# First complex product of two spectral layers in three real products, its activations read one item later

## The chip, the core and the metric

The kernel runs on one core of a Trainium2 chip. The metric is the device time of one execution in microseconds (us), here the median of several executions. The engines are named as in the profile: PE is TensorE (matrix products; PEld is the loading of its stationary operand), DVE is VectorE, ACT is ScalarE, POOL is GpSimd, SP is SyncE, which issues most DMAs. Engines work on tiles in SBUF and PSUM; a product's result arrives in PSUM.

## The reference

Four layers follow one another on an array x of 48 x 48 positions with 768 channels in float32: a transformer block (attention with relative positions, then an MLP), a spectral layer, a scan with a small convolution, and a second spectral layer. The change touches only the two spectral layers, which are the same up to their weights:

```python
xs = jnp.fft.rfft2(xf32, axes=(1, 2)).reshape(B, H, Wm, NUM_HEADS, BLOCK)   # 48 x 25 modes, 8 blocks of 96
xr, xi = jnp.real(xs), jnp.imag(xs)
o1r = relu(einsum('bxyhi,hio->bxyho', xr, w1[0]) - einsum('bxyhi,hio->bxyho', xi, w1[1]) + b1[0])
o1i = relu(einsum('bxyhi,hio->bxyho', xi, w1[0]) + einsum('bxyhi,hio->bxyho', xr, w1[1]) + b1[1])
o2r = einsum('bxyho,hoi->bxyhi', o1r, w2[0]) - einsum('bxyho,hoi->bxyhi', o1i, w2[1]) + b2[0]
o2i = einsum('bxyho,hoi->bxyhi', o1i, w2[0]) + einsum('bxyho,hoi->bxyhi', o1r, w2[1]) + b2[1]
out_c = softshrink(zr, LAMBDA) + 1j * softshrink(zi, LAMBDA)     # zr, zi: o2r, o2i
return jnp.fft.irfft2(out_c, s=(H, W), axes=(1, 2)) + bias       # bias is the layer's input
```

So each of the 8 blocks of 96 channels passes through a complex MLP of two layers, mode by mode. The first of its complex products, xr + i xi with w1[0] + i w1[1], is what the change computes in another way.

## The kernel before, in words

A spectral layer has three stages. First `spectrum_rows` takes the transform along one axis of the picture as products on TensorE and stores it to DRAM (`yu`, one array for each half of the channels). Then `spectrum_mix` takes the transform along the other axis, the MLP, the soft shrinkage and the inverse transform along that axis, and stores back to `yu`. Then the rows are transformed back, in `afno_first` (L1510) for the first spectral layer and `afno_second` (L1541) for the second.

`spectrum_mix` works on items: 2 halves x 5 groups `kc` of KC = 5 modes x 4 blocks of channels, 40 items a layer. G is 48, so an item has n = KC * G = 240 complex columns, or CH = 480 real ones, on 96 partitions (BS). An item passes through four functions:

- `s_fft_h`: five products of 96x96 from the loaded tile `yt` (L1379) give the spectrum in PSUM; ScalarE copies it to `X` in SBUF, real and imaginary part apart (L1381). For the first block of a group it loads `yt` (720 KB) first.
- `s_mlp1`: four products of 96x240 (L1390 to L1393) give real and imaginary part of the first complex product in PSUM, two of them accumulated for each. `w1n` (L1362) holds -w1[1]. ScalarE applies bias and Relu to each part (L1396) into planes 1 and 2 of the tile `o1`; GpSimd writes plane 0 as the negative of plane 2 (L1397).
- `s_mlp2`: ten products of 97x96 (L1407, L1408) with `o1` as the stationary operand give the second complex product, with the bias as a 97th row. The pairs of planes 1, 2 and 0, 1 are the operand for w2[0] and w2[1]. VectorE clamps the result to +-LAMBDA (`cl`, L1411) and subtracts the clamp from it (`Z`, L1413), which is the soft shrinkage.
- `s_ifft_h`: one product of 96x480 (L1422); in the first layer VectorE adds `yt` (L1425), in the second ScalarE and VectorE copy in turn (`ev`, L57 and L59) into `us`, which is stored after the fourth block (L1429).

The order of the instructions is that in which the program emits them; each engine works through its own queue in that order and waits on semaphores for its operands. The order is a software pipeline written out in the last loop: in each step the stages come in reversed order, and stage s works on item step - s.

```python
        stages = [s_fft_h, s_mlp1, s_mlp2, s_ifft_h]
        for step in range(len(items) + len(stages) - 1):
            for s in reversed(range(len(stages))):
```

So TensorE's queue has, step by step, the inverse transform of the item three behind, the second product of the item two behind, the first product of the item one behind, and the forward transform of the new item. Of `o1` there are two tiles in turn, of `X`, `cl`, `Z`, `yt` and `us` two each. PSUM has eight tiles (tag "m") in turn for the whole layer; an item takes four.

Names and lines that matter below: L1322 the products of `spectrum_rows` (f_f), L1353 the load of `yt`, L1033 an add for the scan layer (the tiles `bias` and `u`) whose loads and add lie at the beginning of the first spectral layer's mixing stage, L1158 GpSimd's product in the scan, L1237 its complex products for the rotation, L139 GpSimd's preparation of weights in the transformer block, L564 VectorE's accumulation in the attention, L840 ScalarE's activation in the MLP, L884 GpSimd's add of the MLP's bias.

Of the kernel before, what the change touches and what calls it, by code (L numbers as in the profile page):

```python
# [11 lines left out]
F32 = mybir.dt.float32  # L12
BF16 = mybir.dt.bfloat16
AF = mybir.ActivationFunctionType
ALU = mybir.AluOpType
# [5 lines left out]
G = 48  # L21
# [7 lines left out]
TB = 384  # L29
# [7 lines left out]
NB, BS = 8, 96  # L37
KW = G // 2 + 1
KC = 5
# [95 lines left out]
def combine_right(eng, p, t1, t2, t3, t4):  # L135

    eng.tensor_tensor(t1, p[1], p[0], ALU.subtract)
    eng.tensor_tensor(t3, p[3], p[1], ALU.subtract)
    eng.tensor_tensor(t2, p[3], t1, ALU.subtract)  # L139
    eng.tensor_tensor(t4, p[2], t2, ALU.subtract)  # L140


def block_sums(nc, X, t1, t2, t4):


    blocks = [X[:, k * NC2 : (k + 1) * NC2, n, :] for k in range(2) for n in range(2)]
    combine_right(nc.vector, blocks, t1, t2, blocks[1], t4)
    return blocks[0], blocks[2], t2, t1, blocks[3], blocks[1], t4
# [32 lines left out]
def qkv_phase(tc, ident, x, qkv_w, qkv_b, relT, rel_d, ln_g, ln_b, q_d, k_d, v_d, rw_d, rh_d, wqk_d, wv_d, flag, ahead):  # L181
# [17 lines left out]
    with (  # L199
# [67 lines left out]
        def q_and_k(sb):  # L267
# [3 lines left out]
            for pr in range(NC):  # L271
# [49 lines left out]
                for o, d, m in ((q[:, pr], q_d, qms), (kt, k_d, kms)):  # L321
                    o = o.rearrange("p b t -> p (b t)")
                    nc.scalar.dma_start(d[pr * P : (pr + 1) * P, tok], o)
                    V.tensor_reduce(m[:, pr, sb : sb + 1], o, axis=AX.X, op=ALU.max, apply_absolute_value=True)
                if pr == NC2 and sb + 1 < NSB:
# [33 lines left out]
        with tc.tile_pool(name="qkv_o", bufs=1, side="right") as op:  # L359
# [80 lines left out]
            qm, km = (qp.tile([P, NC], F32, tag=n, name=n) for n in ("qm", "km"))  # L440
            V.tensor_reduce(qm, qms, axis=AX.X, op=ALU.max)
            V.tensor_reduce(km, kms, axis=AX.X, op=ALU.max)
            rm = qp.tile([P, 2], F32, tag="rm", name="rm")
            V.tensor_reduce(rm, rel, axis=AX.X, op=ALU.max, apply_absolute_value=True)
            V.tensor_scalar(km, km, rm[:, 0:1], rm[:, 1:2], ALU.add, ALU.add)
# [881 lines left out]
def spectrum_mix(tc, name, a, layer, yu, psum, keep, side, halves):  # L1327

    nc = tc.nc
    ev = Evac(nc)
    w1, b1, w2, b2 = (a[f"{layer}_{k}"] for k in ("w1", "b1", "w2", "b2"))
    HB = NB // 2
    with (
        tc.tile_pool(name=f"{name}_c", bufs=1, side=side) as cp,
        tc.tile_pool(name=f"{name}_y", bufs=2, side=side) as yp,
        tc.tile_pool(name=f"{name}_s", bufs=2, side=side) as sp,  # L1340
    ):
        fh = cp.tile([BS, BS], F32, tag="fh", name=f"{name}_fh")
        nc.sync.dma_start(fh, a["fh"])
        w1t = cp.tile([BS, NB, 2, BS], F32, tag="w1", name=f"{name}_w1")
        w1n = cp.tile([BS, NB, BS], F32, tag="w1n", name=f"{name}_w1n")
        w2t = cp.tile([BS + 1, NB, 2, BS], F32, tag="w2", name=f"{name}_w2")
        b1t = cp.tile([BS, 2, NB], F32, tag="b1", name=f"{name}_b1")
        ih = cp.tile([BS, BS], F32, tag="ih", name=f"{name}_ih")
        ys = {}

        def load(half, kc):
            yt = yp.tile([BS, KC, TB], F32, tag="yt", name=f"{name}_yt_{half}_{kc}")
            nc.sync.dma_start(yt, yu[half][4 * KC * kc : 4 * KC * (kc + 1)].rearrange("(k q) p c -> (q p) k c", q=4))  # L1353
            us = yp.tile([BS, KC, TB], F32, tag="us", name=f"{name}_us_{half}_{kc}")
            ys[half, kc] = yt, us

        nc.sync.dma_start(w1t, w1)
        nc.sync.dma_start(b1t, b1)
        nc.sync.dma_start(w2t[:BS], w2)
        nc.sync.dma_start(w2t[BS : BS + 1], b2)  # L1360
        nc.sync.dma_start(ih, a["ih"])
        nc.gpsimd.tensor_scalar(w1n, w1t[:, :, 1, :], -1.0, None, ALU.mult)  # L1362

        o1s = []
        for i in range(2):
            o1 = cp.tile([BS + 1, KC, 3, G], F32, tag=f"o1{i}", name=f"{name}_o1{i}")
            nc.vector.memset(o1[BS : BS + 1, :, :, :], 0.0)
            nc.vector.memset(o1[BS : BS + 1, :, 1, :], 1.0)
            o1s.append(o1)
        flow = {}  # L1370

        def s_fft_h(i):
            half, kc, b = items[i]
            if b == 0:
                load(half, kc)
            yt = ys[half, kc][0]
            ps = psum(f"x_{i}")
            for j in range(KC):
                nc.tensor.matmul(ps[:BS, j * BS : (j + 1) * BS], lhsT=yt[:, j, b * BS : (b + 1) * BS], rhs=fh, start=True, stop=True)  # L1379
            X = sp.tile([BS, 2, KC, G], F32, tag="X", name=f"{name}_X_{i}")  # L1380
            nc.scalar.copy(X, ps[:BS, :CH].rearrange("c (k r h) -> c r k h", r=2, h=G))  # L1381
            flow[i] = X

        def s_mlp1(i):
            half, kc, b = items[i]
            b += half * HB
            X = flow[i].rearrange("c r k h -> c r (k h)")
            ps = psum(f"o_{i}")
            n = KC * G
            nc.tensor.matmul(ps[:BS, :n], lhsT=w1t[:, b, 0, :], rhs=X[:, 0, :], start=True, stop=False)  # L1390
            nc.tensor.matmul(ps[:BS, :n], lhsT=w1n[:, b, :], rhs=X[:, 1, :], start=False, stop=True)
            nc.tensor.matmul(ps[:BS, n : 2 * n], lhsT=w1t[:, b, 0, :], rhs=X[:, 1, :], start=True, stop=False)
            nc.tensor.matmul(ps[:BS, n : 2 * n], lhsT=w1t[:, b, 1, :], rhs=X[:, 0, :], start=False, stop=True)  # L1393
            o1 = o1s[i % 2]
            for r in range(2):
                nc.scalar.activation(o1[:BS, :, 1 + r, :], ps[:BS, r * n : (r + 1) * n].rearrange("c (k h) -> c k h", h=G), AF.Relu, bias=b1t[:, r, b : b + 1])  # L1396
            nc.gpsimd.tensor_scalar(o1[:BS, :, 0, :], o1[:BS, :, 2, :], -1.0, None, ALU.mult)  # L1397
            flow[i] = o1

        def s_mlp2(i):  # L1400
            half, kc, b = items[i]
            b += half * HB
            o1 = flow[i]
            ps = psum(f"z_{i}")
            for j in range(KC):
                out = ps[:BS, j * BS : (j + 1) * BS]
                nc.tensor.matmul(out, lhsT=o1[:, j, 1:3, :].rearrange("c r h -> c (r h)"), rhs=w2t[:, b, 0, :], start=True, stop=False)  # L1407
                nc.tensor.matmul(out, lhsT=o1[:, j, 0:2, :].rearrange("c r h -> c (r h)"), rhs=w2t[:, b, 1, :], start=False, stop=True)  # L1408

            cl = sp.tile([BS, CH], F32, tag="cl", name=f"{name}_cl_{i}")  # L1410
            nc.vector.tensor_scalar(cl, ps[:BS, :CH], -LAMBDA, LAMBDA, ALU.max, ALU.min)  # L1411
            Z = sp.tile([BS, CH], F32, tag="Z", name=f"{name}_Z_{i}")
            nc.vector.tensor_tensor(Z, ps[:BS, :CH], cl, ALU.subtract)  # L1413
            flow[i] = Z

        def s_ifft_h(i):
            half, kc, b = items[i]
            Z = flow.pop(i)
            yt, us = ys[half, kc]
            cols = slice(b * BS, (b + 1) * BS)  # L1420
            ps = psum(f"u_{i}")
            nc.tensor.matmul(ps[:BS, :CH], lhsT=ih, rhs=Z, start=True, stop=True)  # L1422
            pv = ps[:BS, :CH].rearrange("p (k c) -> p k c", c=BS)
            if keep:
                nc.vector.tensor_tensor(us[:, :, cols], pv, yt[:, :, cols], ALU.add)  # L1425
            else:
                ev(us[:, :, cols], pv)
            if b == HB - 1:
                nc.sync.dma_start(yu[half][4 * KC * kc : 4 * KC * (kc + 1)].rearrange("(k q) p c -> (q p) k c", q=4), us)  # L1429

        items = [(half, kc, b) for half in halves for kc in range(NKC) for b in range(HB)]
        stages = [s_fft_h, s_mlp1, s_mlp2, s_ifft_h]
        for step in range(len(items) + len(stages) - 1):
            for s in reversed(range(len(stages))):
                i = step - s
                if 0 <= i < len(items):
                    stages[s](i)


def load_spectrum(nc, pool, yu, half, g, name):  # L1440
# [216 lines left out]
```

## Time and profile before

| | before |
|---|---|
| median of three executions | 3971.84 us (3970.29 to 3973.61) |
| profiled execution, span | 3971.0 us |
| mean granted TensorE clock | 0.973 |
| first spectral layer, first copy of X to last inverse transform | 2905.80 to 3123.3 us |
| second spectral layer, the same | 3712.81 to 3926.07 us |

The profile's page gives the busy time of each engine with its share of the span and its count of instructions, then the chain of work that ended last, followed back from the last instruction. The windows of busy time give the same for a stretch of the span. In the timeline a line is a group of neighbouring records of one kind: start and span in us, engine, line, operation, output <- inputs by the program's names, the shapes, the count, and in brackets how long the engine had been idle before and what released it. A float32 product leaves two records. The ends of matmuls are modelled, so starts are the better times for TensorE; spans on GpSimd are rough.

### The profile page before, as it was taken

How to read it: one execution, taken by the hardware profiler on the slowest of the kernel's cores; microseconds unless marked ns; L12 is line 12 of the kernel's file. 1: busy time of each engine (PE TensorE's matmuls, PEld its weight loads, DVE VectorE, ACT ScalarE, POOL GpSimd, SP SyncE). 2: the span in 40 equal slices, each digit the busy share in tenths (PEclk: the TensorE clock that was granted, in tenths of full speed). 3: DMA queues.
4: the chain of work that ended last, by engine and by line, in shares of the span. 5: the costliest groups of instructions: out<-in, count | busy, mean ns of one | idle time of the engine just before them, and what ended most of it. 6: DMA issues, size and time to landing. Idle time of an engine off the chain costs nothing.

```text
span 3971.0 us, 54147 instructions
## 1 busy us (share of the span) xinstructions
PE 3818.7 (96%) x22178; PEld 2329.6 (59%) x22178; DVE 2008.6 (51%) x3020; ACT 1093.3 (28%) x1808; POOL 595.6 (15%) x415
## 2 busy tenths in 40 slices
PE   7999869999999999999999999999989998998998
PEld 4666544444444444455555555555568866995685
DVE  6645446666666666556325233233223268994334
ACT  1323234444434444421210110120022135222331
POOL 3101001101011111034000000000011111971110
PEclk9999989999999999999999999999989799999999
DMA  7666463334232322224335434534434302110434
GB/s 247 195 196 185 157 168 104 101 101 129 78 112 80 104 88 72 86 80 162 106 112 161 142 103 126 156 107 125 128 97 103 94 18 91 38 32 23 144 100 157
DMA packets 262424, 457.24 MB, mean 115 GB/s; under 512 B 32413, under 2 KB 215701, under 8 KB 255799
## 3 DMA queue, kind: packets, MB, share of 16 engines
q1 hardware_dynamic: 251927, 431.07, 36.2%
q10 hardware_dynamic: 10240, 22.61, 1.5%
q8 instruction: 177, 2.90, 0.3%
q14 instruction: 80, 0.66, 0.1%
HBM read 315.31 MB, written 138.31 MB: 114 GB/s over the span
## 4 chain that ended last, share of the span: by engine, by line
PE 71%; issue 10%; DVE 8%; DMA 4%; POOL 3%; ACT 2%; SPq 1%; ACTq 0%; POOLq 0%; DVEq 0%
PE p L845 12%; PE p L908 12%; PE s L546 10%; PE av L575 10%; PE qk L293 6%; PE s L554 4%; PE c L1061 4%; PE v L164 3%; DVE rec L585 2%; PE so L1221 2%; POOL f_o L1397 2%; PE f_w L1510 2%; PE c L1150 1%; PE f_f L1322 1%; DVE s L1170 1%
## 5 line engine op out<-in xcount | busy, mean ns | idle before, releaser
L564 DVE TENSOR_TENSOR acc<-acc,p 128x768 f32<-128x768 f32 x576 | 585.5, 1016 | 357.2 <-ACT p L556 315.5
L556 ACT ACTIVATE p<-s 128x768 f32<-128x768 f32 x648 | 478.6, 812 | 709.3 <-PE s L554 709.3
L546 PE MATMUL s<-qt,kt 64*128 64x384 f32 x2592 | 478.9, 502 | 22.6 <-DVE rest_h L367 21.0
L908 PE MATMUL p<-w,h 128*128 128x384 f32 x1512 | 492.4, 486 | 0.0
L575 PE MATMUL av<-p,vt 128*64 128x384 f32 x2592 | 467.4, 496 | 19.1 <-DVE oT L586 11.5
L908 PEld LDWEIGHTS p<-w,h 128*128 128x128 f32 x1512 | 286.2, 190 | 196.8
L546 PEld LDWEIGHTS s<-qt,kt 64*128 64x128 f32 x2592 | 233.5, 187 | 264.5 <-ACT p L556 88.3
L575 PEld LDWEIGHTS av<-p,vt 128*64 128x64 f32 x2592 | 172.3, 137 | 240.7 <-issue 196.1
L845 PE MATMUL p<-x2nT,w 128*128 128x384 f32 x864 | 293.1, 489 | 0.7 <-issue 0.7
L1150 PE MATMUL c<-H,bands 128*48 128x96 f32 x5632 | 242.7, 247 | 12.3 <-issue 12.3
L554 PE MATMUL s<-bt,oneh 120*128 120x384 bf16 x1296 | 248.2, 328 | 0.0
L1150 PEld LDWEIGHTS c<-H,bands 128*48 128x48 f32 x5632 | 235.5, 124 | 19.7 <-issue 12.7
L293 PE MATMUL qk<-xnT,wqk 128*128 128x384 f32 x756 | 244.8, 486 | 0.0
L845 PEld LDWEIGHTS p<-x2nT,w 128*128 128x128 f32 x864 | 165.0, 191 | 116.4 <-issue 2.9
L845 PE MATMUL p<-xT,w 128*128 128x384 f32 x648 | 220.7, 486 | 0.0
L554 PEld LDWEIGHTS <-oneh 120*128 120x128 bf16 x1296 | 109.1, 98 | 173.6 <-issue 112.2
L293 PEld LDWEIGHTS qk<-xnT,wqk 128*128 128x128 f32 x756 | 143.4, 190 | 99.4
L840 ACT ACTIVATE h<-h,ml_b 128x384 f32<-128x384 f32 x144 | 88.4, 615 | 347.6 <-DVE h L860 176.6
L884 POOL TENSOR_TENSOR rr<-rr,ml_b 128x1152 f32<-128x1152 f32 x12 | 31.7, 2644 | 955.6 <-DMA rr<-xr_d 955.6
L845 PEld LDWEIGHTS p<-xT,w 128*128 128x128 f32 x648 | 123.1, 190 | 85.9
L1158 POOL TENSOR_TENSOR t<-s,c 128x768 f32<-128x768 f32 x80 | 144.8, 1835 | 172.2 <-DVE s L1120 160.5
L1061 PE MATMUL c<-wsc,x2T 128*112 128x357 f32 (+1 forms) x576 | 151.8, 426 | 2.0 <-DVE c L1022 2.0
(298 smaller groups left out, 4678.1 us busy)
## 6 DMA issues: line engine op xcount, KB each, us to landing
w<-w1s_d SPq DMA_DIRECT2D x36, 768.0 KB
w<-w2s_d SPq DMA_DIRECT2D x36, 768.0 KB
bt<-rh_d SPq DMA_DIRECT2D x144, 162.0 KB
w<-w1s_d SPq DMA_DIRECT2D x36, 576.0 KB
w<-in_mlp_w_dram SPq DMA_DIRECT2D x27, 768.0 KB
wqk<-wqk_d SPq DMA_DIRECT2D x12, 1344.0 KB
f_gt<-yu SPq DMA_DIRECT2D x24, 672.0 KB
bt<-rw_d SPq DMA_DIRECT2D x144, 108.0 KB
```

The costliest lines, as they stand in the source:

```text
L164: nc.tensor.matmul(p[:, :TB], lhsT=rhs[n][:, c, t * P : (t + 1) * P], rhs=w[:, c, :], start=c == 0, stop=c == NC2 - 1)
L293: nc.tensor.matmul(p[:, :TB], lhsT=w[:, n, c, :], rhs=ops[sb][n][:, c, :], start=c == 0, stop=c == NC2 - 1)
L546: nc.tensor.matmul(ps[:, s, :QB], lhsT=keys[pr][rows, kt * P : (kt + 1) * P], rhs=chunks[c][0][rows], start=True, stop=False)
L554: nc.tensor.matmul(ps[:, s, :QB], lhsT=oneh[:NBR, b % 3, :], rhs=chunks[c][1][:NBR, s, b // 3, j, :], start=False, stop=True)
L556: nc.scalar.activation(p, ps[:, :, :QB], AF.Exp)
L564: nc.vector.tensor_tensor(probs[c], probs[c], p, ALU.add)
L575: nc.tensor.matmul(avs[c][rows, :QB], lhsT=vals[pr][:, kt, rows], rhs=p[:, s, :], start=kt == 0, stop=kt == NT - 1)
L845: nc.tensor.matmul(p[:, :TB], lhsT=w[n][:, c, :], rhs=rhs[n][:, c, :], start=c == 0, stop=c == NC2 - 1)
L908: nc.tensor.matmul(ps[t][:, :TB], lhsT=hs[left, f][:, t * P : (t + 1) * P], rhs=wt[:, f % KW2, :], start=f == 0, stop=f == NF2 - 1)
L1061: nc.tensor.matmul(ps[:K, i, :n], lhsT=xT[:, cc, tok : tok + K], rhs=w[:, cc, c0 : c0 + n], start=cc == 0, stop=cc == NC - 1)
L1150: nc.tensor.matmul(ps[r0 : r0 + G, k // 4, cols], lhsT=bands[:, n - GC, i, :] if gr else bands0[:, n, i, :], rhs=H[:, n, :, d : d + NPR], ...
L1158: GP.tensor_tensor(t, sc[:, ch], c1[:, m0 : m0 + GC].unsqueeze(2).to_broadcast([P, GC, RR, NPR]), ALU.mult)
```

## The change

With Xs = xr + xi the two parts of the first product can be written with one product in common: real = w1[0].Xs - (w1[0] + w1[1]).xi and imaginary = w1[0].Xs + (w1[1] - w1[0]).xr. That is three real products instead of four, for additions ahead of them and behind them. The change does this for both layers:

- `w1n` is replaced by `w1s` = w1[0] + w1[1] and `w1d` = w1[1] - w1[0], two GpSimd operations of 96x768 a layer instead of one.
- `s_fft_h` has GpSimd add the two parts of `X` into `Xs` (L1384 of the new kernel).
- `s_mlp1` has three products: p2 with Xs (L1394), which needs a PSUM tile of its own, then those with xr and xi (L1395, L1396). ScalarE copies p2 to SBUF (`both`, L1399); VectorE forms the two parts (`pre`, L1400 and L1401) from `both` and the products in PSUM; Relu with bias (L1404) reads `pre` in SBUF instead of PSUM; the negation (L1405) stays.
- The second product works three items behind instead of two, and the inverse transform four instead of three, so that there is a step more between the Relus and their use. Of `o1` there are three tiles in turn, of `yt` three; a layer takes 44 steps instead of 43.

The order of stages within a step, inverse transform, second product, first product, forward transform, stays as it was. On GpSimd the sum Xs of an item comes in the queue behind the negation of the item before. The lines of the later instructions move: second product L1415 and L1416, clamp L1419, Z L1421, inverse transform L1430, add L1433, store L1437, rows of the first layer L1518.

```diff
-        w1n = cp.tile([BS, NB, BS], F32, tag="w1n", name=f"{name}_w1n")
+        w1s, w1d = (cp.tile([BS, NB, BS], F32, tag=n, name=f"{name}_{n}") for n in ("w1s", "w1d"))
...
-            yt = yp.tile([BS, KC, TB], F32, tag="yt", name=f"{name}_yt_{half}_{kc}")
+            yt = yp.tile([BS, KC, TB], F32, tag="yt", name=f"{name}_yt_{half}_{kc}", bufs=3)
...
-        nc.gpsimd.tensor_scalar(w1n, w1t[:, :, 1, :], -1.0, None, ALU.mult)
+        nc.gpsimd.tensor_tensor(w1s, w1t[:, :, 0, :], w1t[:, :, 1, :], ALU.add)
+        nc.gpsimd.tensor_tensor(w1d, w1t[:, :, 1, :], w1t[:, :, 0, :], ALU.subtract)
...
-        for i in range(2):
+        for i in range(3):
             o1 = cp.tile([BS + 1, KC, 3, G], F32, tag=f"o1{i}", name=f"{name}_o1{i}")
...
             nc.scalar.copy(X, ps[:BS, :CH].rearrange("c (k r h) -> c r k h", r=2, h=G))
-            flow[i] = X
+            Xs = sp.tile([BS, KC, G], F32, tag="Xs", name=f"{name}_Xs_{i}")
+            nc.gpsimd.tensor_tensor(Xs, X[:, 0], X[:, 1], ALU.add)
+            flow[i] = X, Xs
...
-            nc.tensor.matmul(ps[:BS, :n], lhsT=w1t[:, b, 0, :], rhs=X[:, 0, :], start=True, stop=False)
-            nc.tensor.matmul(ps[:BS, :n], lhsT=w1n[:, b, :], rhs=X[:, 1, :], start=False, stop=True)
-            nc.tensor.matmul(ps[:BS, n : 2 * n], lhsT=w1t[:, b, 0, :], rhs=X[:, 1, :], start=True, stop=False)
-            nc.tensor.matmul(ps[:BS, n : 2 * n], lhsT=w1t[:, b, 1, :], rhs=X[:, 0, :], start=False, stop=True)
-            o1 = o1s[i % 2]
+            nc.tensor.matmul(p2[:BS, :n], lhsT=w1t[:, b, 0, :], rhs=Xs, start=True, stop=True)
+            nc.tensor.matmul(ps[:BS, :n], lhsT=w1d[:, b, :], rhs=X[:, 0, :], start=True, stop=True)
+            nc.tensor.matmul(ps[:BS, n : 2 * n], lhsT=w1s[:, b, :], rhs=X[:, 1, :], start=True, stop=True)
+            pre = sp.tile([BS, 2, n], F32, tag="pre", name=f"{name}_pre_{i}")
+            both = sp.tile([BS, n], F32, tag="both", name=f"{name}_both_{i}")
+            nc.scalar.copy(both, p2[:BS, :n])
+            nc.vector.tensor_tensor(pre[:, 0], both, ps[:BS, n : 2 * n], ALU.subtract)
+            nc.vector.tensor_tensor(pre[:, 1], both, ps[:BS, :n], ALU.add)
+            o1 = o1s[i % 3]
             for r in range(2):
-                nc.scalar.activation(o1[:BS, :, 1 + r, :], ps[:BS, r * n : (r + 1) * n].rearrange("c (k h) -> c k h", h=G), AF.Relu, bias=b1t[:, r, b : b + 1])
+                nc.scalar.activation(o1[:BS, :, 1 + r, :], pre[:, r].rearrange("c (k h) -> c k h", h=G), AF.Relu, bias=b1t[:, r, b : b + 1])
...
-        stages = [s_fft_h, s_mlp1, s_mlp2, s_ifft_h]
-        for step in range(len(items) + len(stages) - 1):
-            for s in reversed(range(len(stages))):
-                i = step - s
-                if 0 <= i < len(items):
-                    stages[s](i)
+        stages = {s_ifft_h: 4, s_mlp2: 3, s_mlp1: 1, s_fft_h: 0}
+        for step in range(len(items) + 4):
+            for stage, behind in stages.items():
+                if 0 <= step - behind < len(items):
+                    stage(step - behind)
```

More of the change, by code (lines that the diff above doesn't have):

```diff
@@ L1386, in s_mlp1 @@
             b += half * HB
-            X = flow[i].rearrange("c r k h -> c r (k h)")
-            ps = psum(f"o_{i}")
+            X, Xs = (v.rearrange("c r k h -> c r (k h)") if len(v.shape) == 4 else v.rearrange("c k h -> c (k h)") for v in flow[i])
+            ps, p2 = psum(f"o_{i}"), psum(f"o2_{i}")
             n = KC * G
-            nc.tensor.matmul(ps[:BS, :n], lhsT=w1t[:, b, 0, :], rhs=X[:, 0, :], start=True, stop=False)
-            nc.tensor.matmul(ps[:BS, :n], lhsT=w1n[:, b, :], rhs=X[:, 1, :], start=False, stop=True)
-            nc.tensor.matmul(ps[:BS, n : 2 * n], lhsT=w1t[:, b, 0, :], rhs=X[:, 1, :], start=True, stop=False)
-            nc.tensor.matmul(ps[:BS, n : 2 * n], lhsT=w1t[:, b, 1, :], rhs=X[:, 0, :], start=False, stop=True)
-            o1 = o1s[i % 2]
+            nc.tensor.matmul(p2[:BS, :n], lhsT=w1t[:, b, 0, :], rhs=Xs, start=True, stop=True)
[7 more added lines that the diff above has]
+            o1 = o1s[i % 3]
             for r in range(2):
-                nc.scalar.activation(o1[:BS, :, 1 + r, :], ps[:BS, r * n : (r + 1) * n].rearrange("c (k h) -> c k h", h=G), AF.Relu, bias=b1t[:, r, b : b + 1])
+                nc.scalar.activation(o1[:BS, :, 1 + r, :], pre[:, r].rearrange("c (k h) -> c k h", h=G), AF.Relu, bias=b1t[:, r, b : b + 1])
             nc.gpsimd.tensor_scalar(o1[:BS, :, 0, :], o1[:BS, :, 2, :], -1.0, None, ALU.mult)
```

## The prediction, made before the changed kernel ran

> **What bounds the kernel now.** I read the page first, for the whole span:
>
> ```profile
> PE 3818.7 (96%) x22178; PEld 2329.6 (59%) x22178; DVE 2008.6 (51%) x3020; ACT 1093.3 (28%) x1808; POOL 595.6 (15%) x415
> PE 71%; issue 10%; DVE 8%; DMA 4%; POOL 3%; ACT 2%; SPq 1%; ACTq 0%; POOLq 0%; DVEq 0%
> ```
>
> TensorE is busy for 96%, but that is a mean over stages, so I then read the two stretches in which the changed function runs, with the view of busy time by window (columns: sum of the stretch, then busy time of each engine, granted clock, DMA share, GB/s):
>
> ```profile
> 2910.00:3130.00 220.00, 216.80 (x1614) 177.37 (x1613) 79.78 (x122) 54.84 (x121) 34.21 (x41) 0.97 0.29 75
> 3710.00:3930.00 220.00, 215.43 (x1605) 173.85 (x1606) 67.94 (x105) 67.17 (x144) 32.22 (x40) 0.98 0.30 82
> ```
>
> Both spectral layers are on TensorE for 98%; VectorE, ScalarE and GpSimd work for 36, 25 and 16% of the first. DMA is at 0.3. One period of the pipeline in the timeline (start, duration; a group shows the span of its records):
>
> ```profile
> 2936.66 0.57 PE L1390 MATMUL f_o<-f_X,f_w 96*96 96x240 f32 x2
> 2936.86 0.65 DVE L1411 TENSOR_SCALAR f_cl<-f_z 96x480 f32<-96x480 f32 x1 [1.30 <-PE f_z L1408]
> ...
> 2937.55 0.65 DVE L1413 TENSOR_TENSOR f_Z<-f_z,f_cl 96x480 f32<-96x480 f32 x1
> 2937.88 0.57 PE L1393 MATMUL f_o<-f_X,f_w 96*96 96x240 f32 x2
> 2938.28 1.01 PE L1379 MATMUL f_x<-f_fh,f_yt 96*96 96x96 f32 x10
> 2938.54 0.81 ACT L1396 ACTIVATE f_o<-f_o,f_b 96x240 f32<-96x240 f32 x2 [3.84 <-PE f_o L1393]
> 2939.13 0.97 PE L1422 MATMUL f_u<-f_Z,f_ih 96*96 96x480 f32 x2
> ...
> 2939.43 0.81 POOL L1397 TENSOR_SCALAR f_o<-f_o 96x240 f32<-96x240 f32 x1 [4.43 <-ACT f_o L1396]
> 2939.93 0.33 PE L1407 MATMUL f_z<-f_w,f_o 97*96 97x96 f32 x2
> ...
> 2940.28 0.24 PEld L1408 LDWEIGHTS f_z<-f_w,f_o 97*96 97x96 f32 x2 [0.18 <-POOL f_o L1397]
> 2941.89 0.57 PE L1390 MATMUL f_o<-f_X,f_w 96*96 96x240 f32 x2
> ```
>
> From L1390 to L1390 is 5.23 us, and the clamps give the same: item 2 starts at 2926.39, item 39 at 3120.07, 5.235 each. By starts on TensorE: first product 1.62 (four of 0.405), forward transform 0.85, inverse 0.80, second product 1.70 (ten of 0.17), 4.97 in all. The other 0.26 is the second product waiting for the negation L1397.
>
> **What the skill says.** The Trainium skill, "GPSIMD Engine Reference", section 3.1, puts a two-input elementwise add at about 2.6 cycles an element, from a read port that both inputs share. The trace agrees: 936 ns at 384 elements a partition (L1237) and 2644 at 1152 (L884), 2.2 ns an element. "SBUF — State Buffer", section "Who interferes with whom", says that a VectorE instruction with two SBUF inputs contends with a reading GpSimd instruction, and one with at most one SBUF input does not. The trace agrees: L139 takes 1601 ns for 384 elements while L564 adds two SBUF tiles, and L1397, otherwise 0.81, takes 1.33 at 2910.90, the one time that such an add (L1033, 2910.77) runs beside it. "TensorE: Matmul & The Clock Gate", Part 1, has an idle TensorE fall to half clock; here 1.5 us of waiting for Z at the end of the layer are enough: the last inverse takes 1.89 instead of 0.97.
>
> **The change part by part.**
> *Removed:* one product of four, 40 x 0.405 = 16.2 us a layer. The negation now has a step more before its reader, so its stall goes: 38 x 0.26 = 10.0. Together 26.2.
> *New prices.* VectorE 96x240: 554 ns at 384 and 654 at 480 give 0.404 (L1543, L1411). ScalarE copy of 240: 479 and 555 give 0.365. Relu from SBUF: L840 takes 615 at 384, L1396 452 from PSUM at 240; I take 0.50. GpSimd sum Xs of 240: the two rows above give 0.62, the step of 2.34 ns from L1237 to L1158 0.60, L1397's own rate 0.81; I take 0.69. Hand-offs in the trace are 0.03 to 0.09.
> *The loop that the change builds.* On GpSimd, Xs of the next item is queued behind the negation of this one, and TensorE's next p2 (L1394 after) waits for Xs; the transforms and second products behind it in TensorE's queue wait with it. From the start T of p2: the clamp starts at T+0.20, as in the timeline, Z ends at 1.54. Only then does VectorE get to pre0 (1.57 to 1.98) and pre1 (2.01 to 2.42), though the three products are done at 1.38. Second Relu 2.45 to 2.95, negation 3.03 to 3.84, Xs 3.88 to 4.57, next p2 at 4.61 to 4.69. X itself is copied by 3.47 and does not bind; the copy "both" (0.54 to 0.91) hides under Z.
> *Against it TensorE:* 0.80 + 1.70 + 1.215 + 0.85 = 4.565. So GpSimd's round is about as long as TensorE's work, slightly longer. When p2 waits d, the second product before it is done d earlier against T, and Z with it, so the period is 4.69 - d = 4.565 + d: d = 0.065, period 4.63. This costs 2.5 a layer.
> *Fill:* the first p2 waits for Xs (+0.75); the second, with no second product before it yet, for negation and Xs of the round at half clock (about 1.7). 2.4 a layer.
> *Drain:* one step more. Inverse 37 waits 0.3 for Z, inverse 38 the 1.5 that clamp and subtraction take, before the last second product; a last stall of 0.5 that I didn't credit is saved. 1.3, and since such a wait dropped the clock before, inverse 38 and second product 39 take 2.5 more. 3.8 a layer.
> *Entrance:* with three yt and the new tiles the first layer's first load also waits for the last store of the stage before (f1_ys). Before, that wait held the loads of bias and the first X copy to 2905.80, while yt had been asked for at 2889.16. I take the store to land at 2901.6, the load at about 2906, the copy at 2908.1: +2.3 once (bounds 1 and 7). In L3 the waits at the entrance are the same.
> *At nothing:* two GpSimd sums of weights (about 1.8 each for the 2.13 of the negation) lie under the loads before the first item; the five PSUM tiles an item fit in eight; the memset of a third o1 lies before the first load; the third yt is asked for some 25 us ahead; the add of bias, now after the layer, lies beside the 60 us of L1510.
> *Sum:* 2 x (26.2 - 2.5 - 2.4 - 3.8) - 2.3 = 32.7, so 3971.8 - 32.7 = 3939.
>
> **The rivals.**
> (a) GpSimd's round binds clearly. At Xs 1.0 the round is 5.0, and since Z can come only 0.15 earlier before the products (1.38) bind, the period is 4.85: 80 x 0.22 = 17 more, 3956. For it: nine hand-offs in a row, each known to 0.03 or so. Against: the uncontended rows.
> (b) TensorE binds cleanly, period 4.565, and the drain does not cost the clock: 5 and 5 less, 3929; if L1510's 288 matmuls (61.6 us, all at half clock after the drain before) are also released early, up to 30 less, 3900.
> (c) Slower: both GpSimd operations run contended, negation 1.33, Xs 1.0 (1601 x 240/384): round 5.5, period 5.35, 80 x 0.72 = 57 more: 3996. For it: VectorE's load rises by 0.8 an item. Against: clamp, Z, pre and us all have at most one SBUF input, and L1158 keeps its rate beside such work.
>
> **How the numbers follow.** The main case 0.52 (3930 to 3948), (a) 0.23 (3948 to 3964), (b) 0.19 (3900 to 3930), (c) 0.04, and 0.02 for no change. Prediction 3939. The range 3918 to 3956 takes in the main case, two thirds of (a) and half of (b); about 0.2 is left out. Faster 0.93, same 0.03, slower 0.04.
>
> **What would show it.** Period of the clamps 4.6 to 4.65; p2 (L1394) waiting about 0.07 for GpSimd's Xs; L1384 at 0.62 to 0.75; pre0 starting right behind Z; no wait of the second product (L1415/L1416) for the negation; X copy of the first item at 2908; half clock from the wait before inverse 38. Wrong if L1384 or L1405 runs well over 0.8, if "both" or the Relus end later than Z allows, if a yt load is waited for inside a layer, or if the stages between the layers move.

## The result and the profile after

The changed kernel takes 3932.91 us (median of four executions, 3931.08 to 3934.41) against 3972.14 us; the ratio is 0.9901, with a 95% interval of 0.9884 to 0.9918. The prediction was 3939.

The page of the changed kernel, busy time of each engine and then the chain that ended last:

```profile
PE 3773.9 (96%) x22018; PEld 2301.0 (59%) x22018; DVE 2066.0 (53%) x3184; ACT 1116.4 (28%) x1888; POOL 649.0 (17%) x497
PE 81%; DVE 8%; DMA 4%; POOL 2%; issue 2%; ACT 2%; SPq 1%; ACTq 0%; DVEq 0%; POOLq 0%
```

TensorE is busy for 45 us less (the products that are gone are 80 x 0.405 = 32.4 of it) and still for 96% of the span. VectorE is busy for 57 us more, GpSimd for 53: the work has moved to engines that had room. In the chain, "issue" has gone from 10 to 2% and PE up by 10. The chain of the kernel before ran through the negation in the spectral layers, and put down the 4.39 us from one negation to the next as "issue"; now it runs through TensorE there.

One period of the first spectral layer, from the timeline of the changed kernel:

```profile
2937.12 0.57 PE L1394 MATMUL f_o<-f_Xs,f_w 96*96 96x240 f32 x2
2937.32 0.65 DVE L1419 TENSOR_SCALAR f_cl<-f_z 96x480 f32<-96x480 f32 x1 [1.04 <-PE f_z L1416]
...
2937.93 0.57 PE L1396 MATMUL f_o<-f_X,f_w1s 96*96 96x240 f32 x2
2938.01 0.65 DVE L1421 TENSOR_TENSOR f_Z<-f_z,f_cl 96x480 f32<-96x480 f32 x1
2938.34 1.01 PE L1380 MATMUL f_x<-f_fh,f_yt 96*96 96x96 f32 x10
2938.61 0.40 DVE L1400 TENSOR_TENSOR f_pre<-f_both,f_o 96x240 f32<-96x240 f32 x1
2938.93 0.39 DVE L1401 TENSOR_TENSOR f_pre<-f_both,f_o 96x240 f32<-96x240 f32 x1
2939.05 0.88 ACT L1404 ACTIVATE f_o<-f_pre,f_b 96x240 f32<-96x240 f32 x2 [0.91 <-DVE f_pre L1400]
2939.19 0.97 PE L1430 MATMUL f_u<-f_Z,f_ih 96*96 96x480 f32 x2
2940.01 0.81 POOL L1405 TENSOR_SCALAR f_o<-f_o 96x240 f32<-96x240 f32 x1 [3.11 <-ACT f_o L1404]
2940.79 0.69 POOL L1384 TENSOR_TENSOR f_Xs<-f_X 96x240 f32<-96x240 f32 x1
2941.69 0.57 PE L1394 MATMUL f_o<-f_Xs,f_w 96*96 96x240 f32 x2
```

From p2 to p2 is 4.57 us. By the clamps, items 2 to 37 of both layers give 4.572 each. Xs ends at 2941.48, and p2 starts 0.21 later, behind the second product in its own queue: TensorE waits for nothing here. The chain of waits from 2936 to 2947, in the kernel before and then in the changed one, shows the same (a piece that begins or ends outside the stretch is counted whole, so the shares can exceed 100%):

```profile
by line: issue 120.1%; POOL f_o L1397 14.7%; POOLq L1397 0.3%
by line: PE f_z L1416 21.6%; PE f_z L1415 21.6%; PE f_x L1380 15.4%; PE f_u L1430 14.7%; PE f_o L1394 11.1%; PE f_o L1395 9.2%; PE f_o L1396 7.4%
```

The starts of stages in the two traces, taken apart (us):

| stretch | before | after | difference | predicted |
|---|---|---|---|---|
| to the last row product (L1322) of the first spectral layer; nothing there is changed | 2896.2 | 2893.2 | -3.0 | 0 |
| from there to the first copy of X | 9.6 | 12.7 | +3.1 | +2.3 |
| first copy of X to first product of L1510 (L1518 after) | 217.4 | 194.6 | -22.8 | -17.5 |
| that to the first row product of the second spectral layer | 552.9 | 552.0 | -0.9 | 0 |
| from there to its first copy of X | 36.6 | 38.2 | +1.6 | 0 |
| first copy of X to first product of L1541 (L1549 after) | 214.4 | 195.4 | -19.0 | -17.5 |
| to the end | 43.8 | 44.6 | +0.8 | 0 |

The first line is hardly an effect of the change: in the traces of the experiments, most of which have the changed kernel's code up to there, that product starts between 2894.9 and 2898.9. The changed kernel's 2893.2 lies just below all of them. Within a layer, 37 periods save 37 x 0.663 = 24.5 each. What is left of it differs by layer: beginning and end cost 1.7 in the first and 5.5 in the second.

### The profile page after: what moved, and what is told of

It is laid out like the page before. It is cut to its first block, busy times and chain, and to the rows that moved or that the text cites. A ratio compares the mean times of both kernels' runs of the same rounds, so it can differ in the third digit from the quotient of the medians.

```text
span 3930.7 us, 54207 instructions
## 1 busy us (share of the span) xinstructions
PE 3773.9 (96%) x22018; PEld 2301.0 (59%) x22018; DVE 2066.0 (53%) x3184; ACT 1116.4 (28%) x1888; POOL 649.0 (17%) x497
## 4 chain that ended last, share of the span: by engine, by line
PE 81%; DVE 8%; DMA 4%; POOL 2%; issue 2%; ACT 2%; SPq 1%; ACTq 0%; DVEq 0%; POOLq 0%
PE p L845 12%; PE p L908 12%; PE av L575 10%; PE s L546 10%; PE qk L293 6%; PE s L554 4%; PE c L1061 4%; PE pj L164 3%; PE v L164 3%; DVE rec L585 2%; PE f_z L1415 2%; PE f_z L1416 2%; PE f_x L1380 2%; PE f_u L1430 2%; PE so L1221 2%
## 5 line engine op out<-in xcount | busy, mean ns | idle before, releaser
L1150 PE MATMUL c<-H,bands 128*48 128x96 f32 x5632 | 242.6, 247 | 12.5 <-issue 12.3
L1150 PEld LDWEIGHTS c<-H,bands 128*48 128x48 f32 x5632 | 235.5, 124 | 19.8 <-issue 12.7
```

Of the source, the lines that this page charges most:

```text
L1150: nc.tensor.matmul(ps[r0 : r0 + G, k // 4, cols], lhsT=bands[:, n - GC, i, :] if gr else bands0[:, n, i, :], rhs=H[:, n, :, d : d + NPR], ...
```

## The experiments

Four questions: do the lost product and the lost stall each give their own share; who sets the period of the changed kernel; what the beginning and the end of a layer cost, and the clock with them; and what the third yt is for.

### The late use alone

```diff
-        stages = [s_fft_h, s_mlp1, s_mlp2, s_ifft_h]
+        stages = {s_ifft_h: 4, s_mlp2: 3, s_mlp1: 1, s_fft_h: 0}
...
-        for i in range(2):
+        for i in range(3):
...
-            o1 = o1s[i % 2]
+            o1 = o1s[i % 3]
```

(on the kernel before, with the loop over this dictionary and three yt from the changed kernel)

> The old four products, with the new lags (second product three items behind, inverse transform four), three o1 and three yt. My theory (lost product and lost stall each give their own share): the stall of the second product on the negation goes, so the period is TensorE's work of four products, 0.80 + 1.70 + 1.62 + 0.85 = 4.97 us; the 37 steady periods of a layer give 37 x 0.265 = 9.8 back, the longer drain and the entrance of the first layer take some 10 of the 19.6, total about 3962 us. Rival 1 (the later use gives nearly all, the product was hidden): period near 4.57, about 3935. Rival 2 (the stall is not from the lag): period stays 5.235, total 3975 to 3982, the drain alone being paid.

Measured: 3957.3 us (3955.4 to 3964.6), ratio 0.9973 with 0.9938 to 1.0007; the span of its profiled execution is 3961.7. The total alone would not decide it, but the period does: 4.977 us in both layers, where 4.97 was expected. The timeline of that kernel has the second product of an item without a wait for the negation:

```profile
2948.36 0.97 PE L1422 MATMUL f_u<-f_Z,f_ih 96*96 96x480 f32 x2
2948.60 0.81 POOL L1397 TENSOR_SCALAR f_o<-f_o 96x240 f32<-96x240 f32 x1 [4.17 <-PE f_x L1379]
...
2949.17 0.33 PE L1407 MATMUL f_z<-f_w,f_o 97*96 97x96 f32 x2
2949.34 0.33 PE L1408 MATMUL f_z<-f_w,f_o 97*96 97x96 f32 x2
```

L1407 and L1408 follow each other by 0.17; before, 0.35 lay between the first L1407 and the loading for L1408 (2939.93 and 2940.28), with 0.18 of waiting in brackets. So the late use is worth 5.235 - 4.977 = 0.258 a period. The step from here to the changed kernel is 4.977 - 4.572 = 0.405, one product of four.

### The three products alone

```diff
-        stages = {s_ifft_h: 4, s_mlp2: 3, s_mlp1: 1, s_fft_h: 0}
-        for step in range(len(items) + 4):
+        stages = {s_ifft_h: 3, s_mlp2: 2, s_mlp1: 1, s_fft_h: 0}
+        for step in range(len(items) + 3):
```

> The three products with the old lags (second product two items behind, inverse transform three); the rest as in the changed kernel. My theory: from the start T of p2 the second Relu ends at T+2.8, the negation at T+3.7, and the second product's first L1416 comes at T+3.8; 1.53 of it are left then, so the next p2 starts at about T+5.35. The period is longer than before (5.235), 74 x 0.12 = 9 more, with the entrance of the first layer (+3): about 3984 us, slower than the kernel before. Rival (the product's 16 us a layer count by themselves, whatever the lag): about 3942.

Measured: 3987.67 us (3985.97 to 3992.39), ratio 1.0037 with 1.0023 to 1.0051, slower than the kernel before. Period 5.354. Its timeline:

```profile
2936.25 0.57 PE L1394 MATMUL f_o<-f_Xs,f_w 96*96 96x240 f32 x2
...
2938.18 0.88 ACT L1404 ACTIVATE f_o<-f_pre,f_b 96x240 f32<-96x240 f32 x2 [0.91 <-DVE f_pre L1400]
...
2939.13 0.39 PE L1415 MATMUL f_z<-f_w,f_o 97*96 97x96 f32 x2
2939.14 0.81 POOL L1405 TENSOR_SCALAR f_o<-f_o 96x240 f32<-96x240 f32 x1 [3.89 <-ACT f_o L1404]
...
2940.00 0.41 PE L1416 MATMUL f_z<-f_w,f_o 97*96 97x96 f32 x2 [0.48 <-POOL f_o L1405]
```

TensorE reaches the second product 2.9 after p2 and its first L1416 at 3.75, when the negation is done. The shorter first product is paid for by a longer chain of copy, sums, Relus and negation behind it, and by more than it saves. The two parts of the change are not two gains that add up: with the old lag the lost product is a loss of 0.12 a period.

### Less and more work on GpSimd

```diff
-            nc.gpsimd.tensor_scalar(o1[:BS, :, 0, :], o1[:BS, :, 2, :], -1.0, None, ALU.mult)
+            nc.vector.tensor_scalar(o1[:BS, :, 0, :], o1[:BS, :, 2, :], -1.0, None, ALU.mult)
```

> The changed kernel with the negation on VectorE instead of GpSimd, which takes 0.8 us an item out of GpSimd's round of negation, Xs and p2. My theory after the changed kernel's trace (TensorE's own work sets the period, GpSimd's round ends 0.15 to 0.2 before it): no change, period 4.57, 3933 us. Rival (GpSimd's round sets the period, as the prediction's main case had it): the period falls towards 4.5 or below and the total by 5 us or more.

Measured: 3933.69 us (3931.07 to 3936.87), ratio 0.9903 with 0.9886 to 0.9919, which is the changed kernel's; period 4.572. Xs now ends 0.56 before p2 starts, where it was 0.22, and nothing changes: GpSimd's round does not set the period.

```diff
+            Xe = sp.tile([BS, KC, G], F32, tag="Xe", name=f"{name}_Xe_{i}")
+            nc.gpsimd.tensor_tensor(Xe, X[:, 0], X[:, 1], ALU.add)
             nc.gpsimd.tensor_tensor(Xs, X[:, 0], X[:, 1], ALU.add)
```

> The changed kernel with one more GpSimd sum of 96x240 an item (0.69 us, into a tile that nobody reads) ahead of Xs; the result is not changed. GpSimd is then busy for less than half of the period. My theory (GpSimd's round of negation and sums ends only about 0.2 us before TensorE needs Xs): the round becomes 4.40 + 0.69 = 5.09; since p2 waits, Z comes earlier against it and gives up to 0.2 back, so the period is about 4.9 and the total 74 x 0.33 = 24 more, about 3957 us. Rival (GpSimd has two thirds of its time free, so it hides): no change, 3933.

Measured: 3977.48 us (3973.65 to 3982.53), 20 more than expected, and no better than the kernel before; ratio 1.0009, 1.0000 to 1.0018. Period 5.134. Its timeline:

```profile
2936.72 0.70 POOL L1385 TENSOR_TENSOR f_Xe<-f_X 96x240 f32<-96x240 f32 x1
2937.38 0.69 POOL L1386 TENSOR_TENSOR f_Xs<-f_X 96x240 f32<-96x240 f32 x1
2937.83 0.65 DVE L1421 TENSOR_SCALAR f_cl<-f_z 96x480 f32<-96x480 f32 x1 [1.05 <-PE f_z L1418]
2938.12 0.65 PE L1396 MATMUL f_o<-f_Xs,f_w 96*96 96x240 f32 x2 [0.33 <-POOL f_Xs L1386]
...
2939.01 0.57 PE L1398 MATMUL f_o<-f_X,f_w1s 96*96 96x240 f32 x2
2939.69 0.40 DVE L1402 TENSOR_TENSOR f_pre<-f_both,f_o 96x240 f32<-96x240 f32 x1 [0.51 <-PE f_o L1398]
```

Here p2 waits for Xs. GpSimd is busy for less than half of the period and still bounds it, since it waits in turn for Relus that hang on p2. The second sum starts 0.66 after the first, so the round without it is 5.134 - 0.66 = 4.47, which would leave the changed kernel 0.10 us to spare. By its own trace it has somewhat more: p2 starts 0.05 after Xs ends where it waits, and 0.22 after where it doesn't, which is 0.17 to spare and a round of 4.40. The two differ because a p2 that waits takes 0.08 longer to the third product (0.89 for 0.81). My miss was the return of 0.2 through Z. VectorE's first sum starts 0.68 after the third product starts, here (2939.01 to 2939.69) as in the changed kernel (2937.93 to 2938.61); here it had sat idle for 0.51 before. Z coming earlier gives nothing back, because the third product comes no earlier.

### The end of a layer and the clock

At the end the changed kernel waits twice for Z. One step of the order was turned, so that the last second product lies in the first of these waits:

```diff
-            for stage, behind in stages.items():
+            order = list(stages.items())
+            if step == len(items) + 2:
+                order[:2] = order[1::-1]
+            for stage, behind in order:
```

> The changed kernel with the order turned in one step of the drain: in the last step but one the second product of item 39 comes before the inverse transform of item 38, so that it fills the wait for that item's Z. My theory: the wait of 1.43 us before inverse 38 goes, that before inverse 39 falls from 1.52 to about 0.7, and the second product of item 39 runs at full instead of half clock (1.7 less): 3 to 4 us a layer, 3925 to 3927 us. If the clock then stays up into the 288 products of L1518 (60.3 us at half clock), up to 30 less again, about 3897. Rival (the next stage waits for the stored data anyway): no change.

Measured: 3899.82 us (3897.02 to 3901.56), ratio 0.9813 with 0.9797 to 0.9829. One turn in the order brings nearly as much again as the whole change. The wait before inverse 38 is gone, and that before inverse 39 is 0.68. The windows of busy time show where the rest comes from: the drain of the first layer and the rows stage behind it, in the changed kernel (the last three fields are granted clock, DMA share and GB/s)

```profile
3094.50:3097.50 3.00, 3.00 (x18) 2.66 (x17) 0.65 (x1) 0.00 (x0) 0.00 (x0) 0.50 0.00 0
3098.00:3101.00 3.00, 1.48 (x9) 0.94 (x8) 1.61 (x3) 0.00 (x0) 0.00 (x0) 1.00 0.00 0
3101.00:3161.00 60.00, 60.00 (x285) 60.00 (x284) 9.85 (x19) 8.62 (x18) 12.87 (x4) 0.50 0.44 129
```

and with the turned step:

```profile
3095.00:3102.00 7.00, 6.10 (x48) 4.39 (x47) 5.10 (x10) 1.07 (x3) 0.81 (x1) 1.00 0.00 1
3103.00:3135.00 32.00, 31.86 (x286) 31.73 (x284) 9.92 (x19) 8.62 (x18) 12.88 (x4) 1.00 0.91 241
```

In the changed kernel the first wait (1.43, to 3093.76) brought the clock to half for some 3 us and the second (1.52, to 3099.64) for good. At the beginning of the rows stage, 3100.49, the clock was still at full; it fell within the first microsecond of it. The same 288 products take 60.5 us there and 32.4 at full clock. In both cases TensorE is busy nearly the whole time; being busy did not bring the clock back. From the first copy of X to the next stage the turned step saves 2.8 in the first layer (194.6 to 191.8); in the second layer the stretch from the first row product to the next stage is 4.3 shorter (233.6 to 229.3).

To tell the clock from the order, the changed kernel kept its order and got products that nobody reads into its waits:

```diff
+            if i >= len(items) - 2:
+                for k in range(2):
+                    nc.tensor.matmul(psum(f"warm_{i}_{k}")[:BS, : 4 * BS], lhsT=ih, rhs=w1t[:, 2 * k % NB : 2 * k % NB + 2].rearrange("c b r o -> c (b r o)"), start=True, stop=True)
             cols = slice(b * BS, (b + 1) * BS)
             ps = psum(f"u_{i}")
```

> The changed kernel in its own order, with two products of 96x384 that nobody reads (0.65 us each) put into TensorE's queue ahead of each of the last two inverse transforms of a layer, where it waits 1.4 and 1.5 us for Z. No wait is taken away. Theory A (the waits of the drain drop the clock, and the first layer's rows then stay at half clock for 60 us): L1518's stage takes some 32 us, and the total is 3933 - 28 - 3 = about 3902. Theory B (the turned order of the drain experiment moved something else, as the placement of the next stage's loads): no gain, 3933 to 3934.

Measured: 3903.61 us (3901.55 to 3904.56), ratio 0.9823 with 0.9807 to 0.9840. The two waits are down to 0.23 each, and the rows stage runs at full clock:

```profile
3103.00:3135.00 32.00, 31.83 (x283) 31.49 (x281) 9.55 (x19) 8.62 (x18) 12.89 (x4) 1.00 0.92 242
```

And the kernel before, with the same two products only ahead of the very last inverse transform (`if i == len(items) - 1`):

> The kernel before with two such products ahead of the last inverse transform of each layer, in the wait of 1.5 us. Theory A: its rows stage L1510 falls from 61 to some 32 us too, total about 3942 us, with nothing of the change in it. Theory B: no gain, 3972. If A holds, the gain of the drain is owed to neither part of the change, and the change is worth the same 40 us on top of it.

Measured: 3942.25 us (3939.86 to 3945.61), ratio 0.9919 with 0.9902 to 0.9935. Its window of the rows stage:

```profile
3125.00:3157.00 32.00, 31.65 (x280) 31.28 (x279) 9.54 (x18) 8.48 (x18) 12.88 (x4) 1.00 0.90 221
```

Of the two products the trace has one at 3119.42, in the wait for the last negation, and one at 3121.67, in the wait for Z, which falls from 1.52 to 0.88. The clock is the cause, in both kernels: a wait of 1.5 us, in part filled with work of no use, is worth 30 us. The change is worth the same with it (3942.25 to 3903.61, 38.6 us) as without (39.2). So this gain belongs to neither part of the change.

### The beginning of a layer

```diff
+            if keep and i == 0:
+                for k in range(10):
+                    nc.tensor.matmul(psum(f"warm_{i}_{k}")[:BS, : 4 * BS], lhsT=ih, rhs=w1t[:, 2 * k % NB : 2 * k % NB + 2].rearrange("c b r o -> c (b r o)"), start=True, stop=True)
             ps = psum(f"x_{i}")
```

> The changed kernel with the turned drain, and ten products of 96x384 that nobody reads ahead of the first item of the first layer, while TensorE waits some 10 us for the first load. Theory (the fill of the first layer runs at half clock only because TensorE was idle before it): the first item's forward transform takes 1.0 instead of 1.9, the stretch from there to the third p2 some 3 us less, total about 3896 against 3900 without. Rival (the loads or GpSimd set the fill): no gain.

Measured: 3903.5 us (3897.96 to 3908.88), ratio 0.9820 with 0.9803 to 0.9836. The ten products ended 2.8 us before the load came, and the first transform ran for 1.89, at half clock as before, so this run doesn't decide between the two. In its profiled execution the rows stage also took 39.3 us, at full clock up to 3125, then at 0.71 and 0.50: TensorE had waited for 1.25 us, until 3125.45, for the load of f_gt. With fourteen:

> The turned drain with fourteen instead of ten unread products ahead of the first item of the first layer, so that they reach to within about 0.3 us of the first load's landing, where ten left TensorE idle for 2.8 us and the clock at half. Theory: the first forward transform takes about 1.0 instead of 1.9 and the stretch from the first copy of X to the third p2 falls from 12.9 to about 10 us; total about 3896 where the clock holds in L1518's stage. Rival (GpSimd's round and the Relus set the fill): the stretch stays near 12.9.

Measured: 3897.94 us (3896.86 to 3905.1), ratio 0.9815 with 0.9798 to 0.9831. Its timeline:

```profile
2898.09 9.24 PE L1380 MATMUL f_warm<-f_w,f_ih 96*96 96x384 f32 x28 [0.74 <-DVE f_ys L59]
...
2907.81 1.06 PE L1383 MATMUL f_x<-f_fh,f_yt 96*96 96x96 f32 x10 [0.48 <-DMA f_yt<-yu]
...
2910.28 1.11 PE L1397 MATMUL f_o<-f_Xs,f_w 96*96 96x240 f32 x2 [1.41 <-POOL f_Xs L1387]
```

The first transform is at full clock now, 1.06. But the next product waits 1.41 for the copy and Xs and runs at half clock again, for 1.11, and from the first copy of X to the third p2 it is 13.1 us. In the other runs with this fill that stretch is 12.9 (the changed kernel) to 14.4 (the turned kernel, on which this one is built, has 14.3), so a microsecond is not decided here; the 3 us of the theory did not come. The fill's own waits remain, and the rival held. Whether the clock could be kept by filling those too was not tried.

### The third yt

```diff
-            yt = yp.tile([BS, KC, TB], F32, tag="yt", name=f"{name}_yt_{half}_{kc}", bufs=3)
+            yt = yp.tile([BS, KC, TB], F32, tag="yt", name=f"{name}_yt_{half}_{kc}")
```

> The changed kernel with two yt tiles in turn instead of three. My theory: in the first layer the load for a group can then only be asked for when the adds of the group two before are done, some 6.6 us before its first use; store and load of 720 KB each keep the DMA engines for about 6.3 us from that point, so that the wait is 0 to 0.5 us a group, at most 4 us in the layer; in the second layer nothing waits. If the third yt is also what makes the first load wait for the last store of the stage before, the first copy of X comes some 3 us earlier. Total 3929 to 3937 us. Rival (the later inverse transform makes the third yt necessary): each of the eight groups waits 3 us or more, 3955 or more.

Measured: 3952.47 us, with a wide spread (3933.01 to 3959.23) whose cause stays open, ratio 0.9939 with 0.9913 to 0.9966. The view of waits on TensorE for the first layer (total, times, longest, in us):

```profile
PE f_x L1380 <- DMA f_yt<-yu: 13.1, 8, 1.9
```

Eight groups wait up to 1.9 us, more than the 0.5 that I allowed and less than the rival's 3. From item 2's clamp to item 39's the first layer takes 186.6 us instead of 170.0, 16.6 more; the second layer keeps its 4.57. So the third yt is needed in the layer where the input is added at the end. The reason, by the code, is that the later inverse transform, with whose result yt is added, holds a yt for a step longer. It is not what makes the first load wait: with two yt the load is still issued 4.0 us after the last store of the stage before (2897.80 to 2901.80), as with three (2894.34 to 2898.34). Nor are the tiles for the sums needed for that wait: the late use alone, which has none of them, shows it too (2900.46 to 2904.45). Of the new tiles only the third o1 is in both of these kernels; it was not tried by itself.

## Why the prediction was right

- *The gain of a period* was right to the last step. Product: 0.405 predicted, 0.405 measured between the late use alone and the changed kernel. Stall: 0.26 predicted, 0.258 measured.
- *The loop on GpSimd* was mis-sized. The prediction has p2 waiting 0.065 for Xs, a period of 4.63; in fact p2 waits for nothing, the period is TensorE's 4.572 (4.565 predicted for a clean bound), and the round is 4.40 to 4.47 instead of 4.69. So for the period rival (b) came true; its other half, a drain that keeps the clock, did not. The price of Xs was right (0.69, measured 0.687). What failed is the adding up of whole durations of small operations in a row: the next one starts before the recorded end of the one ahead. The first sum starts 1.49 after p2, not 1.57; from there to the end of the second Relu it is 1.32, not 1.38; Xs starts 0.78 after the negation starts, not 0.85. Together 0.21, by which Xs ends earlier (4.36 after p2, not 4.57). It was worth 37 x 0.06 = 2 us a layer.
- *The way through Z* failed with it. The prediction has the first sum wait for Z, and a late p2 win time back through an earlier Z. In the kernel with the second sum Z does come earlier, 0.55 against the first sum, and the first sum still starts 0.68 after the third product.
- *Rival (a)*, GpSimd clearly binding, did not come true, but by 0.10 to 0.17 us only; the second sum shows what it would have looked like. *Rival (c)*, contention: L1384 takes 0.684 to 0.692 and L1405 0.804 to 0.808 in all 80 items, so there is none, as the Trainium skill ("SBUF — State Buffer", section "Who interferes with whom") has it for VectorE operations with at most one SBUF input.
- *Fill and drain* were right in sum for one layer and too dear for the other. I take the time of a stretch less TensorE's work in it at full clock (products 1.62 or 1.215, transforms 0.85 and 0.80, second product 1.70). From the first copy of X to the third first product, before 15.16 - 9.14 = 6.0 in the first layer and 12.7 - 9.14 = 3.5 in the second, after 12.9 - 5.83 = 7.1 in both: the fill costs 1.1 and 3.6 more, where 2.4 each was predicted. From the last first product to the next stage, before 8.6 - 4.92 = 3.7 and 8.05 - 4.92 = 3.1, after 12.5 - 7.02 = 5.5 and 13.3 - 7.02 = 6.3: the drain costs 1.8 and 3.2, where 3.8 each was predicted. Together 6.8 of 6.2 in the second layer, 2.9 of 6.2 in the first. Much of the difference between the layers is the clock. In the fill it came back to full some 11 us after the first copy of X in the first layer of the kernel before and in both layers of the changed one, but some 6 us after it in the second layer of the kernel before; five more microseconds at half clock cost some 2.5, by estimate. In the first layer that kernel's negation also ran beside the add L1033 for 1.33, and the add has moved out of the layer. In the drain of the changed kernel's first layer the clock was at full again for the last inverse (1.02 us), while in the second layer that inverse took 1.89. These are single executions, and the first stretch varies from 12.9 to 14.4 in the runs with this fill.
- *Entrance*: +2.3 predicted, +3.1 measured.
- *The rows of the first layer* (L1510, L1518 after) stayed at half clock nearly throughout. That it could be released early was given as the tail of rival (b), "up to 30 less"; the turned step then showed 28.

The forecast came out 6 us too high (3939 against 3933). The two layers together gave 6.8 us more than forecast (41.8 against 35.0), 4 of them from the loop and most of the rest from the fill and drain of the first layer; the other stretches balance to within 1 us. That they do is luck: the -3.0 of the first stretch, where nothing was changed, offsets what the others cost. And that the total lies in the range of the main case does not confirm its loop, since 5 us separate it from the clean bound; the traces decide that.

## What to carry to other kernels

When an engine at 98% loses work, first write down the next loop through the other engines: here three products without the later use were slower than four, and the later use alone brings two fifths of what a period gains (0.258 of 0.663). An engine that is busy for a third of the time can be within 0.2 us of bounding the kernel, if it stands in a chain that closes on itself. And look at the clock behind every drain: a wait of 1.5 us at the end of one stage set the speed of the next one for 60 us.

## What the runs showed of the hardware

- Half clock can be a lasting state of a busy TensorE. The Trainium skill ("TensorE: Matmul & The Clock Gate", Part 1) has the clock go up after some 3.4 us of sustained activity and fall after an idle window of about that length. Here waits of 1.4 and 1.5 us were enough to bring it down, and in the 288 products of 100x128 by 96 columns TensorE was busy for 60.00 of 60.00 us and stayed at 0.50. In this stage the measurement differs from the page; what makes the difference (the loads of weights between short products, perhaps) was not tried. It is not so in every stage: in the rows of the second layer (L1549), entered at 0.50 at 3886.1, the clock is 1.00 from 3890 to 3919.
- To enter the rows stage of the first layer at full clock is not enough to keep it. Where the last wait ahead of it was 0.68 or 0.88 us, the clock stayed up (the turned kernel, the kernel before with two added products). After one of 1.52 the changed kernel entered the stage at full clock and lost it within a microsecond. Not each such wait does it: in the second layer of the late use alone one of 1.52, to 3912.86, left the clock at 1.00 (3908 to 3918).
- In all, 3 of 37 executions of the kernel before took 3939.75 to 3944.82 us, where the others take 3968 to 3978. That is just what it takes with the clock kept (3942.25). Their mean granted clock is 0.980 to 0.981, that of the others 0.970 to 0.974, and that of the kernel with the two added products 0.981 to 0.982. So the clock stayed up in those too; that it did so in the rows stage, and by chance, is likely but not shown, since they left no trace.
- At full clock the rows stage comes to its next limit: DMA is at 0.90 to 0.92 of its share, and a late load can drop the clock again, as the execution with ten added products shows (a wait of 1.25 us; the stage took 39.3).
- The same negation of 96x240 takes 0.81 on GpSimd and 0.30 on VectorE (2939.47, L1405 of that experiment), while a sum of two tiles of that size takes GpSimd 0.69.
